# Four graph layers on 128 graphs: bias added in PSUM, scores and attention turned by way of DRAM, a new timetable, and a rearranged start

## The chip, the cores and the metric

The kernel runs on one core of a Trainium2 chip. The engines are TensorE (PE, with PEld for its weight loads), VectorE (DVE), ScalarE (ACT), GpSimd (POOL) and SyncE (SP), which here only issues DMAs. Each engine takes its own instructions in order and waits on semaphores for the others. The metric is the device time of one execution in microseconds (us), lower is better.

## The reference

`x` is 128 graphs of 128 nodes with 512 features, `adj` a 128x128 matrix shared by all graphs. Four layers follow each other; each ends in `x = layernorm(x + layer(x))` over the features.

```python
# layer 0
y = einsum('nm,bmd->bnd', adj, x);  out = y @ W0 + bias
# layer 1
q, k, v = x @ Wq.T, x @ Wk.T, x @ Wv.T
rel = adj.T * (q @ k.T);  rel /= norm(rel, axis=2);  out = rel @ v
# layer 2
h = x @ W2;  s1, s2 = h @ a1, h @ a2
e = leaky_relu(s1[:, :, None] + s2[:, None, :], 0.2) * adj
out = elu(softmax(e, axis=2) @ h + beta * h)
# layer 3 (with W1 = W2 = adj the row's own term drops out of the difference C - A)
out = relu(max over features of adj @ x + b)        # one number per node
```

All of it is in fp32.

## The kernel before, in words

The 128 graphs are handled in 32 groups of G = 4. For each group the kernel makes the same chain of steps, and the steps of about four groups are interleaved. The order is written out by hand: every step is handed to `emit(at, f)` with a time in slots, `TABLE` (lines 231 to 246) gives the times of a group, 28 slots apart from group to group, `FIRST` (248) changes them for groups 0 and 1 and `LAST` (250) for groups 29, 30 and 31. At the end all pieces are sorted by their time (line 826) and called in that order. So the table sets the order of the instructions on every engine; no scheduler moves them afterwards, and each engine works through its queue in that order.

Names in the profile, with the steps that make them:

- `load` reads a group's `x` (tile x1). `aggregate` multiplies by `adjT` (p_y) and ScalarE copies the result to yT.
- `product` (339) multiplies a group's 512x512 block matrix by a weight matrix with seven products of half-size blocks instead of eight (two by two blocks, sums of blocks as factors). The sums on the data side (s_y, s_x, s_z) are made by GpSimd in `left_factors` (294), those of the weights once, by VectorE, in `weight_blocks` (143). The seven steps go in `ORDER = (1, 2, 6, 5, 7, 3, 4)`; their results lie in three PSUM regions, r0 (two buffers) and r1 and r2, which share one buffer (tag r12). After each step `out` (359) drains the region: a copy by ScalarE or an addition by VectorE. A region is added to by the next step of its number, so that step waits for the drain. Four products of this kind are made per group: r_y (layer 0), r_m (x times Wq^T Wk, layer 1), r_v (layer 1) and r_z (layer 2).
- `biased` (434): GpSimd adds the bias row to x1, so that the drains of r_y add onto it.
- `turn_blocks` and `move` transpose x for layer 1: VectorE transposes 32x32 blocks (xB), and 16 DMAs put the blocks in place (xT). Groups 0 and 1 use TensorE (`turn`, p_xT) instead. `turn_rel` and `move_rel` do the same with the masked scores (relB, relT).
- `scores` (p_rel), `masked`, `squares`, `inverse`, `attend` (p_o), `residual`: the rest of layer 1. `dots` and `scale_dots` compute the two dot products of layer 2 for each node (d12).
- `spread` (623): four TensorE transposes (p_s) put the second dot product of every node on all partitions. `leaky` (632), `weighted` (643, GpSimd), `greatest` (646), `exps` (650, ScalarE), `divide` (662, GpSimd multiplies by the reciprocal): the softmax. `turn_att` (669): four TensorE transposes (p_eT); `with_beta` (675) adds beta times the identity and writes eT. `gather` (685): p_z from x2 and eT.
- `exp`, `elu`, `widen` (p_a), `top`, `norm`, `store`: the end of layer 2 and layer 3.

PSUM tiles of whole banks (p_y, p_rel, p_z and so on) share three buffers (`bank`, line 82).

Before group 0 the weights are loaded, W0, the bias and W2 by ACT's DMA queue, the rest by SP's. `prepare_qk` (163) computes Wq^T Wk with 16 plain 128x512 products (p_m), `prepare_v` (178) transposes Wv (p_wv), and `prepare_dots` (188) and `prepare_rows` (202) make the rows for the two dot products (col, wa).

Of the kernel before, what the change touches and what calls it, by code (L numbers as in the profile page):

```python
# [8 lines left out]
FP = mybir.dt.float32  # L9
# [20 lines left out]
def kernel(  # L30
# [32 lines left out]
    nc = tc.nc  # L63
# [8 lines left out]
    G = 4  # L72
    NG = B // G
    assert B % G == 0 and K == 4

# [3 lines left out]
    small = ctx.enter_context(tc.tile_pool(name="small", bufs=4))  # L79
    psum = ctx.enter_context(tc.tile_pool(name="psum", bufs=1, space=bass.MemoryType.PSUM))  # L80

    def bank(name):
        return psum.tile([P, D], FP, tag="ps", name=name, bufs=3)
# [21 lines left out]
    bias_sb = const.tile([P, D], FP)  # L105
    nc.scalar.dma_start(bias_sb, on_all(bias0, D))

# [34 lines left out]

    def weight_blocks(w, name, keep=0):


        def blk(kh, ch):
            return w[:, 2 * kh : 2 * kh + 2, H * ch : H * ch + H]

        t = const.tile([P, 3 + keep, 2, H], FP, name=f"t_{name}")
        t2, t3, t4 = t[:, 0], t[:, 1], t[:, 2]  # L150
        t1 = t[:, 3] if keep else blk(0, 1)
        dve.tensor_tensor(t3, blk(1, 1), blk(0, 1), ALU.subtract)
        dve.tensor_tensor(t2, t3, blk(0, 0), ALU.add)
        dve.tensor_tensor(t4, blk(1, 0), t2, ALU.subtract)
        dve.tensor_tensor(t1, blk(0, 1), blk(0, 0), ALU.subtract)
        return {1: blk(0, 0), 2: blk(1, 0), 3: blk(1, 1), 4: t4, 5: t1, 6: t2, 7: t3}

    bw = {}

    def prepare_0():  # L160
        bw["0"] = weight_blocks(w0_sb, "0")

    def prepare_qk(c):

        pm = bank(f"p_m{c}")
        for e in range(K):
            pe.matmul(
                pm,
                wq_sb[:, e, c * P : (c + 1) * P],
                wk_sb[:, e, :],  # L170
                start=(e == 0),
                stop=(e == K - 1),
            )
        act.copy(m_qk[:, c, :], pm)
        if c == K - 1:
            bw["m"] = weight_blocks(m_qk, "m")

    def prepare_v(c):
        pv = bank(f"p_wv{c}")
        for e in range(K):  # L180
            pe.transpose(pv[:, e * P : (e + 1) * P], wv_sb[:, e, c * P : (c + 1) * P], ident)
        act.copy(wvT[:, c, :], pv)
        if c == K - 1:
            bw["v"] = weight_blocks(wvT, "v")

# [27 lines left out]

    def prepare_2():
        bw["2"] = weight_blocks(w2_sb, "2", 1)


# [9 lines left out]
    def row(at, step, n=G):  # L227
# [110 lines left out]

    def product(at, name, mul, s, w, c, fresh, begin=None):


        r = {}

        def step(i):
# [4 lines left out]
            if first:  # L349
                r[where] = psum.tile(  # L350
                    [P, 2, H],
                    FP,
                    tag="r0" if where == 0 else "r12",
                    name=f"r{where}_{name}",
                    bufs=2 if where == 0 else 1,
                )
            mul(r[where], s["f"][i], bw[w][i], first)
# [7 lines left out]

        for n, i in enumerate(ORDER):
            emit(at[n], step, i)
            emit(at[n] + 0.72, out, i)
# [46 lines left out]
    def layer0(g, t):  # L415
# [24 lines left out]
        each(t["bias"], biased)  # L440
        left_factors(t["y_sums"], s, "yT", "s_yz", f"y_{g}", 0)
        product(t["y_w"], f"y_{g}", by_rows, s, "0", rows_of(lambda: x1[g]), False)
        each(t["stats0"], lambda b: stats(s, f"0_{g}", b, x1[g][:, b, :]))
# [176 lines left out]
    def layer2(g, t):  # L620
        s = {}

        def spread():
            s["p"] = bank(f"p_s2_{g}")
            for b in range(G):
                pe.transpose(
                    s["p"][:, b * P : (b + 1) * P],
                    s12[g][:, 1, b : b + 1].to_broadcast([P, P]),
                    ident,
                )  # L630

        def leaky():
            e = work.tile([P, G, P], FP, tag="e", name=f"e_{g}")
            dve.tensor_tensor(
                e,
                s["p"].rearrange("p (b n) -> p b n", b=G),
                s12[g][:, 0, :, None].to_broadcast([P, G, P]),
# [24 lines left out]
        def divide(i):  # L662
            rs = small.tile([P, n], FP, tag=f"rs{n}", name=f"rs_{g}_{i}")
            dve.reciprocal(rs, s["sums"][:, i * n : i * n + n])
            e = s["e"][:, i * n : i * n + n, :]
            engine = pool if n == G else dve
            engine.tensor_tensor(e, e, rs[:, :, None].to_broadcast([P, n, P]), ALU.mult)
# [7 lines left out]
        def with_beta(i):  # L675
            if i == 0:
# [5 lines left out]
                ALU.add,  # L682
            )

        def gather(b):
# [52 lines left out]
        each(t["divide"], divide)  # L738
        each(t["turn_att"], turn_att)
        each(t["with_beta"], with_beta)  # L740
        each(t["gather"], gather)
# [115 lines left out]
```

## Time and profile before

| | |
|---|---|
| time, three runs | 2218.19, 2218.97, 2220.17 us |
| the profiled run, and its span | 2217.06 us, 2214.6 us |
| busy: PE, DVE, ACT, POOL | 2170.9, 1547.9, 1102.5, 907.7 us |
| 16 DMA engines, q1 | 19.7% |
| granted TensorE clock, mean | 0.996 |
| GpSimd's bias additions | x128, 1331 ns each |
| TensorE transposes p_s and p_eT | x128 each |

Busy times are unions: two instructions of one engine that overlap count once. A matmul on fp32 data appears as two records, a transpose as one. Spans of matmuls include the way through the array and so overlap; what one costs in a row is the distance from start to start. In a timeline the columns are the start in us, the length in us, engine, line, operation, output and inputs, shapes and the number of instructions that were merged; brackets give the idle time of the engine just before and what ended it.

### The profile page before, as it was taken

To read this page: it belongs to the slowest core of one execution; us is meant where nothing else is said; L and a number is where in the kernel's file an instruction comes from. 1 tells how busy PE (TensorE), PEld (TensorE's weight loads), DVE (VectorE), ACT (ScalarE), POOL (GpSimd) and SP (SyncE) were. 2 spreads that over 40 slices of the span, in tenths; PEclk is the share of its full clock that TensorE was granted. 3 is DMA by queue.
4 is the path that set the end of the run, shared out by engine and by line. 5 is a ranking of instruction groups with operands and counts; after the bars stand their busy time and mean duration, and the time that the engine had idled before them with its cause. 6 is when DMAs were issued, how large, how long until landed. Compare 5 with 4: busy or idle time off the path is not lost.

```text
span 2214.6 us, 31863 instructions
## 1 busy us (share of the span) xinstructions
PE 2170.9 (98%) x11073; PEld 1839.6 (83%) x11073; DVE 1547.9 (70%) x3290; ACT 1102.5 (50%) x2446; POOL 907.7 (41%) x743
## 2 busy tenths in 40 slices
PE   7999999999999999999999999999999999999996
PEld 5788888888888888888888888888888888888873
DVE  4657766767766767776767776767767677667676
ACT  2224445554445554445554445554455554455547
POOL 3334444334444344443344443344443344443321
PEclk9999999999999999999999999999999999999998
DMA  4011222211222211222112222112222112221101
GB/s 167 25 20 29 61 60 62 62 20 49 60 60 63 58 21 52 59 61 62 44 31 56 58 62 63 41 30 59 58 62 63 29 39 62 59 63 44 21 28 57
DMA packets 333295, 115.15 MB, mean 52 GB/s; under 512 B 297424, under 2 KB 297552, under 8 KB 333136
## 3 DMA queue, kind: packets, MB, share of 16 engines
q1 hardware_dynamic: 331936, 110.77, 19.7%
q10 hardware_dynamic: 1200, 2.36, 0.3%
q8 instruction: 88, 1.44, 0.3%
q14 instruction: 71, 0.58, 0.1%
HBM read 39.65 MB, written 33.55 MB: 33 GB/s over the span
## 4 chain that ended last, share of the span: by engine, by line
PE 93%; DVE 3%; ACT 2%; POOL 1%; issue 1%; DMA 0%; ACTq 0%; DVEq 0%; POOLq 0%
PE r_y L26 17%; PE r_v L26 17%; PE r_m L26 17%; PE r_z L26 17%; PE p_z L26 5%; PE p_rel L26 5%; PE p_y L26 5%; PE p_o L26 5%; PE p_a L26 5%; DVE x L26 1%; ACT x L26 1%; DVE st L26 1%; PE p_eT L26 1%; PE p_m L26 1%; PE p_s L26 1%
## 5 line engine op out<-in xcount | busy, mean ns | idle before, releaser
L26 ACT ACTIVATE x<-x,nmean,rstd 128x512 f32<-128x512 f32 x384 | 288.6, 808 | 120.8 <-DVE nmean L26 120.8
L26 DVE BATCH_NORM_STATS2 st<-x 128x6 f32<-128x512 f32 x384 | 263.8, 687 | 8.8
L26 POOL TENSOR_TENSOR x<-x,bias_sb 128x512 f32<-128x512 f32 x128 | 170.1, 1331 | 137.9 <-PE p_y L26 137.5
L26 DVE SCALAR_TENSOR_TENSOR x<-m,x 128x512 f32<-128x512 f32 x128 | 114.4, 894 | 108.5 <-ACT m L26 98.5
L26 POOL TENSOR_TENSOR s_x<-xT 128x512 f32<-128x512 f32 x64 | 82.2, 1285 | 261.1 <-DMA xT<-xB 250.2
L26 ACT COPY c<-r_z 128x512 f32<-128x512 f32 x124 | 71.2, 574 | 223.3 <-PE r_z L26 198.0
L26 ACT COPY yT<-p_y 128x512 f32<-128x512 f32 x128 | 75.1, 586 | 213.6 <-PE p_y L26 213.6
L26 POOL TENSOR_TENSOR rstd<-ve,mhalf 128x4 f32<-128x4 f32 (+1 forms) x99 | 98.5, 995 | 194.1 <-DVE ve L26 188.9
L26 DVE TENSOR_TENSOR x<-r_y,x 128x512 f32<-128x512 f32 x224 | 151.7, 678 | 31.2 <-PE r_y L26 31.0
L26 DVE SCALAR_TENSOR_TENSOR scr<-x,wa 128x512 f32<-128x512 f32 x256 | 161.5, 675 | 0.0
L26 DVE STREAM_TRANSPOSE xB<-x 128x512 f32<-128x512 f32 x120 | 81.2, 696 | 108.7 <-ACT x L26 97.7
L26 PEld LDWEIGHTS p_y<-adjT,x 128*128 128x128 f32 x1024 | 136.9, 196 | 11.2 <-ACT adjT L26 4.8
L26 POOL TENSOR_TENSOR s_z<-zT 128x512 f32<-128x512 f32 x31 | 39.4, 1270 | 255.9 <-ACT zT L26 255.9
L26 PE MATMUL p_y<-adjT,x 128*128 128x128 f32 x1024 | 137.6, 280 | 4.5 <-ACT adjT L26 4.5
L26 PEld LDWEIGHTS p_z<-eT,x 128*128 128x128 f32 x1024 | 134.0, 192 | 7.9 <-issue 1.0
L26 PEld LDWEIGHTS p_rel<-xT,tT 128*128 128x128 f32 x1024 | 134.1, 191 | 7.4 <-DVE tT L26 0.8
L26 DVE TENSOR_REDUCE mx<-p_a 128x1 f32<-128x512 f32 x128 | 88.3, 691 | 69.6 <-PE p_a L26 69.6
L26 PE MATMUL p_a<-x,adjT 128*128 128x512 f32 x256 | 130.8, 596 | 5.8 <-DVE mx L26 4.4
L26 ACT COPY tT<-r_m 128x512 f32<-128x512 f32 x128 | 75.6, 590 | 121.6 <-PE r_m L26 121.6
L26 PE MATMUL p_rel<-xT,tT 128*128 128x128 f32 x1024 | 134.9, 275 | 0.6 <-DVE tT L26 0.6
L26 PE MATMUL p_z<-eT,x 128*128 128x128 f32 x1024 | 134.7, 275 | 0.1
L26 PE MATMUL p_o<-v,relT 128*128 128x512 f32 x256 | 130.4, 593 | 0.3 <-ACT v L26 0.3
(129 smaller groups left out, 5268.6 us busy)
## 6 DMA issues: line engine op xcount, KB each, us to landing
out_dram<-x SPq DMA_DIRECT2D x128, 256.0 KB, 2.5
x<-in_x_dram SPq DMA_DIRECT2D x31, 1024.0 KB, 5.3
xT<-xB SPq DMA_DIRECT2D x480, 64.0 KB, 2.3
relT<-relB SPq DMA_DIRECT2D x512, 16.0 KB, 1.8
w_sb<-in_L_gnn_weight_dram ACTq DMA_DIRECT2D x1, 1024.0 KB, 5.6
x<-in_x_dram SPq DMA_DIRECT2D x4, 256.0 KB, 7.8
wq_sb<-in_L_gnn_Wq_dram SPq DMA_DIRECT2D x1, 1024.0 KB, 12.3
wk_sb<-in_L_gnn_Wk_dram SPq DMA_DIRECT2D x1, 1024.0 KB, 15.1
```

The costliest lines, as they stand in the source:

```text
L26: return lambda *args, **kw: self.tc.keep_in_program_order(op(*args, **kw))
```

## The change

What it does:

1. **Bias.** `biased` is gone. Two ScalarE copies per group (`fill`) put the bias into regions r0 and r2 before the first step that writes there (0.7 slots before steps 1 and 5), and these steps add onto it. `bias_sb` holds the left half of the bias and the right half less the left. Three opening matmuls write each region's buffers once.
2. **Scores.** For groups 0 to 29 `spread` writes the column of d12 to DRAM and reads it back on all partitions (s2d, s2), two DMAs on SP, in place of p_s. Groups 30 and 31 keep TensorE.
3. **Attention.** For groups 0 to 29 `divide` is done by VectorE with beta added in the same instruction, four per group; a block transpose (eB), one DMA to DRAM and four DMAs back (eT) take the place of p_eT and `with_beta`.
4. **New times** for y_sums, spread to divide, exp to store, and the first two groups.
5. **The fill.** The bias and W2 are loaded by SP's queue. VectorE copies adjT. Eight warm-up matmuls. Wq^T Wk is made by `product`, with factors of wk (t_k) and wq (s_q). The factors of the weights are emitted one by one at times of their own, those of W2 earlier; xT of group 0 and the transposes of Wv are interleaved.

The diff, cut to its core:

```diff
-    nc.scalar.dma_start(bias_sb, on_all(bias0, D))
+    nc.sync.dma_start(bias_sb, on_all(bias0, D))
...
-    nc.scalar.dma_start(w2_sb, w2.rearrange("(k p) f -> p k f", p=P))
+    nc.sync.dma_start(w2_sb, w2.rearrange("(k p) f -> p k f", p=P))
...
+    bias_halves = {0: bias_sb[:, :H], 2: bias_sb[:, H:]}
+    dve.tensor_tensor(bias_halves[2], bias_halves[2], bias_halves[0], ALU.subtract)
     ident = const.tile([P, P], FP)
     make_identity(nc, ident)
+    for tag, n in (("r0", 2), ("r12", 1)):
+        for i in range(n):
+            r = psum.tile([P, 2, H], FP, tag=tag, name=f"first_{tag}_{i}", bufs=n)
+            pe.matmul(r, ident, ident[:, None, :].to_broadcast([P, G, P]), start=True, stop=True)
     mhalf = const.tile([P, G], FP)
     dve.memset(mhalf, -0.5)
 
     adjT = const.tile([P, P], FP)
     pt = bank("p_adjT")
     pe.transpose(pt[:, :P], adj_sb, ident)
-    act.copy(adjT, pt[:, :P])
+    dve.tensor_copy(adjT, pt[:, :P])
+    warm = bank("p_warm")
+    for i in range(WARM):
+        pe.matmul(warm[:, :P], ident, ident, start=True, stop=True)
     adj_b = adj_sb[:, None, :].to_broadcast([P, G, P])
     adjT_b = adjT[:, None, :].to_broadcast([P, G, P])
 
...
-        load=[-20], y=row(0.5, 1), bias=row(1.3, 1), y_sums=row(5.2, 0.5), y_w=row(7, 1, 7),
+        load=[-20], y=row(0.5, 1), y_sums=row(4.3, 0.5), y_w=row(7, 1, 7),
...
-        spread=[61.6], leaky=[62.0], weighted=[63.4], greatest=[64.3], exps=[64.4],
-        divide=[65.8], turn_att=[68.6], with_beta=[69.0], gather=row(71.5, 1),
-        z_sums=row(75.3, 0.5), z_w=row(77, 1, 7), exp=[87.5, 88.5, 90.4, 92.0],
-        elu=[87.8, 89.4, 92.8, 93.8], norm2=[95.0], apply2=row(95.7, 0.33),
-        widen=[98.7, 100.0, 103.6, 104.6], top=[99.1, 100.4, 104.0, 105.0],
-        stats3=[99.8, 101.1, 104.7, 105.7], norm3=[106.2], apply3=row(107, 0.33), store=[108.5],
+        spread=[57.3], leaky=[62.6], weighted=[62.9], greatest=[63.9], exps=[64.0],
+        divide=[65.2], turn_att=[68.6], with_beta=[69.0], turn_blocks_2=[65.7], move_2=[65.8], gather=row(71.5, 1),
+        z_sums=row(75.3, 0.5), z_w=row(77, 1, 7), exp=[86.0, 87.0, 96.0, 99.6],
+        elu=[86.4, 87.4, 96.8, 100.3], norm2=[101.4], apply2=row(102.4, 0.33),
+        widen=[104.2, 104.9, 105.6, 106.3], top=[104.7, 105.4, 106.1, 106.8],
+        norm3=[107.4], apply3=row(108.4, 0.33), store=[109.8],
     )
 
...
-    FIRST = {0: dict(turn=row(20.4, 0.3)), 1: dict(y=row(-9.5, 0.3), bias=row(-9.2, 0.3))}
+    FIRST = {
+        0: dict(stats0=row(15.8, 0.02), norm0=[15.95], apply0=row(18.0, 0.1), turn=row(20.4, 0.3)),
+        1: dict(y=row(-9.5, 0.3), turn=row(20.3, 0.3), x_sums=row(22.5, 0.5)),
+    }
...
+        def fill(where):
+            r[where] = region(where)
+            act.copy(r[where], before[where][:, None, :].to_broadcast([P, 2, H]))
...
+            if first and before is not None and where in before:
+                first = False
+            elif first:
+                r[where] = region(where)
...
+            if before is not None and i in (1, 5):
+                emit(at[n] - 0.7, fill, REGION[i])
...
-        def biased(b):
-            pool.tensor_tensor(x1[g][:, b, :], x1[g][:, b, :], bias_sb, ALU.add)
...
+                line = dram.tile([P, G], FP, tag="s2", name=f"s2d_{g}")
+                sync.dma_start(line, s12[g][:, 1, :])
+                wide = work.tile([P, P, G], FP, tag="s2", name=f"s2_{g}")
+                sync.dma_start(
+                    wide.rearrange("p n b -> p (n b)"),
+                    line.rearrange("n b -> (n b)")[None, :].to_broadcast([P, P * G]),
+                )
...
+            if not late:
+                for b in range(G):
+                    e = s["e"][:, b, :]
+                    dve.scalar_tensor_tensor(
+                        e, e, rs[:, b : b + 1], beta_i, op0=ALU.mult, op1=ALU.add
+                    )
+                return
...
+        def turn_blocks():
+            s["eB"] = work.tile([P, Q, G, P // Q], FP, tag="eB", name=f"eB_{g}")
+            dve.transpose(
+                s["eB"].rearrange("p q b u -> p b q u"),
+                s["e"].rearrange("p b (q u) -> p b q u", q=Q),
+            )
+
+        def move():
+            m = P // Q
+            blocks = dram.tile([P, Q, G * m], FP, tag="eB", name=f"eBd_{g}")
+            sync.dma_start(blocks, s["eB"].rearrange("p q b u -> p q (b u)"))
+            eT = work.tile([P, Q, G, m], FP, tag="eT", name=f"eT_{g}")
+            for q in range(Q):
+                sync.dma_start(
+                    eT[q * m : (q + 1) * m].rearrange("p a b u -> p a (b u)"),
+                    blocks.rearrange("(a j) q n -> q j a n", a=Q)[q],
+                )
+            s["eT"] = eT.rearrange("p a b u -> p b a u")
...
-    emit(-1, prepare_0)
-    each(row(14.0, 1.0), prepare_qk)
-    each(row(18.0, 0.1), prepare_v)
-    each(row(29.2, 1.8), prepare_dots)
-    emit(40.7, prepare_rows)
-    emit(61.0, prepare_2)
+    weight_blocks(row(-1, 0), "0", w0_sb)
+    weight_blocks([11.85, 11.86, 12.85, 12.86], "k", wk_sb, 1, "x2")
+    qk = {"qT": wq_sb}
+    left_factors(row(12.0, 0.1), qk, "qT", "s_x", "q", 1)
+    product(row(14, 1, 7), "qk", by_rows, qk, "k", rows_of(lambda: m_qk), True)
+    weight_blocks([19.8, 19.81, 20.9, 20.91], "m", m_qk)
+    each(row(21.0, 0.1), prepare_v)
+    weight_blocks(row(29.8, 0.01), "v", wvT)
+    each([33.8, 34.2, 43.8, 44.8], prepare_dots)
+    emit(49.0, prepare_rows)
+    weight_blocks(row(48.9, 0.01), "2", w2_sb, 1)
```

In 'late' groups (30 and 31) `spread`, `turn_att` and `with_beta` are as before.

More of the change, by code (lines that the diff above doesn't have):

```diff
@@ L73 @@
     NG = B // G
+    WARM = 8
     assert B % G == 0 and K == 4
@@ L80 @@
     psum = ctx.enter_context(tc.tile_pool(name="psum", bufs=1, space=bass.MemoryType.PSUM))
+    dram = ctx.enter_context(tc.tile_pool(name="dram", bufs=2, space=bass.MemoryType.DRAM))
     def bank(name):
@@ L141, with weight_blocks, factor @@
     beta_b = beta_i[:, None, :].to_broadcast([P, G, P])
-    def weight_blocks(w, name, keep=0):
+    def weight_blocks(at, key, w, keep=0, tag=None):
         def blk(kh, ch):
             return w[:, 2 * kh : 2 * kh + 2, H * ch : H * ch + H]
[L149 to L156, printed above, removed]
-    bw = {}
[L160 to L176, printed above, removed]
+        t = {}
+        def factor(i):
+            if i == 0:
+                home, args = (const, {}) if tag is None else (data, dict(tag=tag))
+                u = home.tile([P, 3 + keep, 2, H], FP, name=f"t_{key}", **args)
+                t.update({2: u[:, 0], 3: u[:, 1], 4: u[:, 2]})
+                t[1] = u[:, 3] if keep else blk(0, 1)
+                bw[key] = {
+                    1: blk(0, 0), 2: blk(1, 0), 3: blk(1, 1), 4: t[4], 5: t[1], 6: t[2], 7: t[3],
+                }
+            to, left, op, right = (
+                (3, blk(1, 1), ALU.subtract, blk(0, 1)),
+                (2, t[3], ALU.add, blk(0, 0)),
+                (4, blk(1, 0), ALU.subtract, t[2]),
+                (1, blk(0, 1), ALU.subtract, blk(0, 0)),
+            )[i]
+            dve.tensor_tensor(t[to], left, right, op)
+        for i in range(4):
+            emit(at[i], factor, i)
+    bw = {}
     def prepare_v(c):
@@ L182, in prepare_v @@
         act.copy(wvT[:, c, :], pv)
-        if c == K - 1:
-            bw["v"] = weight_blocks(wvT, "v")
     col = const.tile([P, 2, K], FP)
@@ L212, in prepare_rows @@
         dve.tensor_scalar(beta_i, ident, beta_sb, None, op0=ALU.mult)
-    def prepare_2():
-        bw["2"] = weight_blocks(w2_sb, "2", 1)
     pieces = []
@@ L239 @@
         apply1=row(65.4, 0.33),
-        spread=[61.6], leaky=[62.0], weighted=[63.4], greatest=[64.3], exps=[64.4],
-        divide=[65.8], turn_att=[68.6], with_beta=[69.0], gather=row(71.5, 1),
-        z_sums=row(75.3, 0.5), z_w=row(77, 1, 7), exp=[87.5, 88.5, 90.4, 92.0],
-        elu=[87.8, 89.4, 92.8, 93.8], norm2=[95.0], apply2=row(95.7, 0.33),
-        widen=[98.7, 100.0, 103.6, 104.6], top=[99.1, 100.4, 104.0, 105.0],
-        stats3=[99.8, 101.1, 104.7, 105.7], norm3=[106.2], apply3=row(107, 0.33), store=[108.5],
-    )
-    FIRST = {0: dict(turn=row(20.4, 0.3)), 1: dict(y=row(-9.5, 0.3), bias=row(-9.2, 0.3))}
+        spread=[57.3], leaky=[62.6], weighted=[62.9], greatest=[63.9], exps=[64.0],
[4 more added lines that the diff above has]
+        norm3=[107.4], apply3=row(108.4, 0.33), store=[109.8],
+    )
+    FIRST = {
+        0: dict(stats0=row(15.8, 0.02), norm0=[15.95], apply0=row(18.0, 0.1), turn=row(20.4, 0.3)),
+        1: dict(y=row(-9.5, 0.3), turn=row(20.3, 0.3), x_sums=row(22.5, 0.5)),
+    }
     LAST = {
@@ L337, in by_columns, with product, region @@
                 )
-    def product(at, name, mul, s, w, c, fresh, begin=None):
+    def product(at, name, mul, s, w, c, fresh, begin=None, before=None):
         r = {}
+        def fill(where):
+            r[where] = region(where)
+            act.copy(r[where], before[where][:, None, :].to_broadcast([P, 2, H]))
+        def region(where):
+            return psum.tile(
+                [P, 2, H],
+                FP,
+                tag="r0" if where == 0 else "r12",
+                name=f"r{where}_{name}",
+                bufs=2 if where == 0 else 1,
+            )
         def step(i):
@@ L348, in step @@
             first = i in (1, 2, 5)
[L349 to L356, printed above, removed]
+            if first and before is not None and where in before:
+                first = False
+            elif first:
+                r[where] = region(where)
             mul(r[where], s["f"][i], bw[w][i], first)
@@ L439, in layer0 @@
         each(t["y"], aggregate)
-        each(t["bias"], biased)
         left_factors(t["y_sums"], s, "yT", "s_yz", f"y_{g}", 0)
-        product(t["y_w"], f"y_{g}", by_rows, s, "0", rows_of(lambda: x1[g]), False)
+        product(
+            t["y_w"], f"y_{g}", by_rows, s, "0", rows_of(lambda: x1[g]), False, before=bias_halves
+        )
         each(t["stats0"], lambda b: stats(s, f"0_{g}", b, x1[g][:, b, :]))
@@ L621, in layer2 @@
         s = {}
+        late = g >= NG - 2
         def spread():
[L624 to L629, printed above, removed]
+            if late:
+                p = bank(f"p_s2_{g}")
+                for b in range(G):
+                    pe.transpose(
+                        p[:, b * P : (b + 1) * P],
+                        s12[g][:, 1, b : b + 1].to_broadcast([P, P]),
+                        ident,
+                    )
+                s["s2"] = p.rearrange("p (b n) -> p b n", b=G)
+            else:
+                line = dram.tile([P, G], FP, tag="s2", name=f"s2d_{g}")
[4 more added lines that the diff above has]
+                    line.rearrange("n b -> (n b)")[None, :].to_broadcast([P, P * G]),
                 )
+                s["s2"] = wide.rearrange("p n b -> p b n")
         def leaky():
@@ L635, in leaky @@
                 e,
-                s["p"].rearrange("p (b n) -> p b n", b=G),
+                s["s2"],
                 s12[g][:, 0, :, None].to_broadcast([P, G, P]),
@@ L664, in divide @@
             dve.reciprocal(rs, s["sums"][:, i * n : i * n + n])
+            if not late:
+                for b in range(G):
+                    e = s["e"][:, b, :]
[3 more added lines that the diff above has]
+                return
             e = s["e"][:, i * n : i * n + n, :]
@@ L683, in with_beta @@
             )
+        def turn_blocks():
[3 more added lines that the diff above has]
+                s["e"].rearrange("p b (q u) -> p b q u", q=Q),
+            )
+        def move():
[7 more added lines that the diff above has]
+                    blocks.rearrange("(a j) q n -> q j a n", a=Q)[q],
+                )
+            s["eT"] = eT.rearrange("p a b u -> p b a u")
         def gather(b):
@@ L738, in layer2 @@
         each(t["divide"], divide)
-        each(t["turn_att"], turn_att)
-        each(t["with_beta"], with_beta)
+        if late:
+            each(t["turn_att"], turn_att)
+            each(t["with_beta"], with_beta)
+        else:
+            emit(t["turn_blocks_2"][0], turn_blocks)
+            emit(t["move_2"][0], move)
         each(t["gather"], gather)
```

## The prediction

> **What bounds the kernel now.** I read the page's busy times first, then its chain of waits, then one period by the windows view and the timeline, and last the timeline of the first 130 us. The page, parts 1 and 4:
>
> ```profile
> PE 2170.9 (98%) x11073; PEld 1839.6 (83%) x11073; DVE 1547.9 (70%) x3290; ACT 1102.5 (50%) x2446; POOL 907.7 (41%) x743
> ...
> PE 93%; DVE 3%; ACT 2%; POOL 1%; issue 1%; DMA 0%; ACTq 0%; DVEq 0%; POOLq 0%
> ```
>
> TensorE is busy nearly always, and the chain that ends last runs on it. An average over stages can mislead, so here is one period (a group of four batch elements), by engine, in the middle of the run:
>
> ```profile
> core 0: us, PE busy (x) PEld busy (x) DVE busy (x) ACT busy (x) POOL busy (x), PEclk, DMA share, GB/s
> ...
> 922.29:989.10 66.81, 66.81 (x345) 57.15 (x344) 48.65 (x102) 34.22 (x76) 28.14 (x24) 1.00 0.21 52
> ```
>
> 66.81 us of 66.81: no idle time on TensorE at full clock, 18 us of idle on VectorE, 32 on ScalarE. The sum agrees: 28 steps of the four seven-product multiplications start 1.727 us apart (48.4), twelve 128-column blocks take 0.89 (10.7), eight 512-column ones 0.86 (6.9), two sets of transposes 0.437 (0.9). So in the steady part only work taken from TensorE, or a new wait put on it, counts. The two sets are these, each read from its own start to the next start (the 0.60 includes the pipeline's drain):
>
> ```profile
> 920.78 0.60 PE L26 MATMUL p_s<-ident,d 128*128 128x128 f32 x4
> 921.22 1.89 PE L26 MATMUL r_m<-xT,t_m 128*128 128x256 f32 x8
> ...
> 802.60 0.60 PE L26 MATMUL p_eT<-ident,e 128*128 128x128 f32 x4
> 803.04 1.89 PE L26 MATMUL r_y<-t,yT 128*128 128x256 f32 x8
> ```
>
> The fill is different: there TensorE waits, and what it waits for is in brackets.
>
> ```profile
> 8.41 6.55 PE L26 MATMUL p_y<-adjT,x 128*128 128x128 f32 x32 [4.46 <-ACT adjT L26]
> ...
> 56.70 1.99 PE L26 MATMUL r_m<-s_x,t_m 128*128 128x256 f32 x8 [2.00 <-POOL s_x L26]
> ...
> 112.25 2.97 PE L26 MATMUL r_m<-s_x,m_qk 128*128 128x256 f32 x8 [4.39 <-DVE tT L26]
> ...
> 125.61 1.99 PE L26 MATMUL r_y<-w_sb,yT 128*128 128x256 f32 x8 [1.46 <-DVE tT L26]
> ```
>
> **The Trainium skill.** "TensorE: Matmul & The Clock Gate", Part 1: the array runs at half rate until it has been busy for about 3.4 us, and falls back after such a time idle. The trace agrees: the first 32 records take 6.55 us where later ones take 3.6, and after the 4.39 us wait eight records take 2.97 instead of 1.89. "SBUF — State Buffer", Who interferes with whom: a VectorE instruction with two SBUF inputs and a GpSimd one that reads SBUF exclude each other for a whole instruction. It agrees:
>
> ```profile
> 852.69 1.27 POOL L26 TENSOR_TENSOR s_y<-s_y,yT 128x512 f32<-128x512 f32 x1
> 852.82 1.69 DVE L26 SCALAR_TENSOR_TENSOR x<-c,x 128x512 f32<-128x512 f32 x1
> ```
>
> 1.69 instead of 0.68. [...] the page shows 1.8 to 2.5 for 16 to 256 KB. "PSUM — Partial Sum Buffer", The four PSUM rules: ScalarE writes do not change the bits that decide whether a matmul adds or overwrites; a matmul adds to ScalarE's data where an earlier one left the bit set. That is what the three opening matmuls are for; the trace before has no such case.
>
> **The change, part by part (steady state).**
> Scores and attention by DRAM, for groups 0 to 29: 2 x 30 sets x 0.437 us leave TensorE, 26.2 us. Nothing else on TensorE changes per group.
> The scores' way now: a write of 2 KB and a broadcast read of 256 KB on SP, about 2 x 2.5 us, so 5 from the end of the d12 row. That row ends 11.0 us before the group's first y step (call that moment 0; every time in the next paragraphs is relative to it), so the row is back at -6; its reader, leaky, stands behind the last two tT adds and cannot start before -0.9. Hidden, with 5 us to spare. On SP it stands behind four output stores and ahead of the load for a later group (20 slots early) and of the attention's DMAs; none of these is due.
> The attention's way: on VectorE four scalar_tensor_tensor of 128x128 (about 0.28 each, the nearest row is relB at 0.283) and one 32x32-block transpose (0.70, row xB) come, the eT add (0.67) goes: +1.2 us. GpSimd loses its multiply (1.05). On SP one 256 KB write whose landing the next four reads wait for: 2.5, then four issues of 0.65 and 2.3 to land, 7.4 us. The transpose ends at about 8.2, so eT is there at 15.6; p_z wants it at 19.1. Behind it on SP stand the sixteen relT moves, due when VectorE has relB at 13.9, while SP is through at 13.3. Hidden.
> Bias into PSUM: 4 GpSimd adds per group (5.3 us) go, two ScalarE copies (0.58 each, as c<-r_z) come. ScalarE is at half load. The first fill stands early (-3.9). The second is the edit's risk: it waits for VectorE to drain region 1 after step 2 (done 4.6), and in ScalarE's order it is behind the four exps, which wait for greatest, which waits for GpSimd's weighted, which waits for leaky. Worked out: tT done -0.9; leaky's first op now has two SBUF inputs and is shut out by yT until -0.55, then to 0.05; its second is shut out by s_y and ends at 1.85; weighted 3.2; greatest 4.0; exps (1.65) 5.75; fill 6.4. TensorE wants it after y1, y2, p_rel, y6, p_rel: 3 x 1.727 + ... = 6.96. So 0.5 us spare, and TensorE loses nothing. With both shut-outs at full length it is 6.9: at worst some 0.1 us. Bounds for this edit: 0 to +0.6 per group (a gain is excluded, since TensorE has no idle time to give).
> New times: p_a and elu move; after v, p_a, z and o I find every drain ahead of its next writer, the nearest being v's fifth step, copied at 27.1 for the step at 27.9. Zero.
>
> **The fill.** (Absolute times.) bias_sb moves from ACT's queue to SP's, behind x; the last x landed at 10.71 with the same bytes ahead, so take bias at 10.7. VectorE subtracts its halves (0.35), and only then copies adjT: p_y starts near 11.5, not 8.41. If the eleven warm-up matmuls keep the clock up it takes 3.6 us: 15.1, against 14.8. ScalarE then puts the last yT and the fill (2 x 0.59) ahead of y: 16.4. Seven steps: 28.5 against 27.84. Wq^T Wk: 7 x 1.727 = 12.1 for 13.7; p_y of group 1 (3.6) now lies inside it, and covers the additions for t_m; then transposes of x and Wv through three banks, paced by eight ScalarE copies: 48.7. Then m without the 2.0 us wait: 60.8, against 65.44. y of group 1 15.7, v 12.1 plus a wait of some 1.6 (v's fifth copy behind three normalisations on ScalarE), xT, wa and p_o 6.1: 96.3 against 99.83. Then group 1's m meets the long VectorE chain of group 0's residuals and dots as before (15.0 us from the first residual to tT); without GpSimd's bias adds the three small d operations need 0.6 instead of 3.7, so 12, from 94: TensorE waits 2.7, not 4.39, and likely keeps its clock. y of group 2 starts near 115, against 122.25, of which 0.44 is a transpose already counted: 6.8. The 1.46 us wait in it came from w2's factors, now made earlier: 1.4 more. Fill: -8.2; bounds +2 (p_y cold, every bank wait longer) to -13.
> The end of the run (from 2109 on) keeps its order of work: 0, at most 2 either way.
>
> **Sum.** 2214.6 - 26.2 - 8.2 = 2180.2 us for the span. That profiled execution was 2217.06 as a run, and the three runs have the median 2218.97, 4.4 above the span; so 2185.
>
> **Rivals.** (A) The fill gains nothing: late p_y, cold clock, and ScalarE as pacemaker take back what the shorter products give. For it: p_y does start 3 us later. Then 2219 - 26 = 2193.
> (B) The second fill comes late by a little in every group: 0.3 to 0.6 us x 30 = 9 to 18: 2194 to 2203. For it: four engines in a row with half a microsecond to spare. Against it: in the trace before the same chain from leaky to exps repeats within 0.1 us from group to group.
> (C) Slower, one mechanism: the same fill at y5, with leaky delayed enough (its strided read of the row s2, or the lock lost twice more). Price: each period loses what the chain is late beyond 0.5 us. It decides from 0.5 + 34/30 = 1.65 us on; at 2.1 us late TensorE waits 1.6 x 30 = 48: 2185 + 48 = 2233. Against it: p_s is read at 0.68 and the SBUF transposes with strided sides show no surcharge (0.70).
> (D) The scores never get off TensorE's path, since the DRAM round trips take over 10 us in place of 5 to 7: p_z or leaky would wait, the transposes' saving is eaten, 2215 to 2222. Against it: 2.5 us landings at 20% DMA share.
>
> **How the numbers follow.** My forecast 0.60, A 0.12, B 0.13, C 0.12, D 0.03. What the measurement can tell from no change is 0.2%, 4.4 us. Faster: forecast, A and B, 0.85; D gives 0.02 of same and 0.01 of slower; C 0.12: slower 0.13. The range: the fill's good bound gives 2180 less some in the tail, so 2174 below; above through A and B to 2204. C and D stay out, 0.15.
>
> **What would show it.** Right: period 65.93 with TensorE without idle time; no p_s or p_eT before group 30; POOL busy near 700 us, ACT near 1140; r_y's fifth-product step without a wait for ACT. Wrong: a bracket "<-ACT r_y" on that step in every group (B, C); p_z waiting for DMA eT (D); y of group 2 starting after 120 (A).

## The result, and the profile after

The changed kernel takes 2187.68 us (median of four runs, 2185.98 to 2189.60) against 2218.58 for the kernel before: ratio 0.986, 95% interval 0.9843 to 0.9877. The forecast was 2185. The two runs near 2186 were granted 0.996 of the clock and the two near 2189.5 were granted 0.994 and 0.995, so a difference of 2 to 4 us between medians is read below together with the traces. The profiled execution ran 2189.29 us with a span of 2187.4, 27.2 less than before. Its page, parts 1 and 4 (the lines of the kernel before are in the prediction):

```profile
PE 2152.3 (98%) x10879; PEld 1823.8 (83%) x10879; DVE 1557.2 (71%) x3419; ACT 1127.9 (52%) x2509; POOL 722.4 (33%) x589
...
PE 94%; DVE 3%; ACT 1%; issue 1%; DMA 0%; POOL 0%; SPq 0%; ACTq 0%; DVEq 0%
```

TensorE has 18.6 us less busy time and the same share of it; GpSimd has lost 185 us and ScalarE gained 25. One period by the windows view, from the y of one group to the y of the next:

```profile
core 0: us, PE busy (x) PEld busy (x) DVE busy (x) ACT busy (x) POOL busy (x), PEclk, DMA share, GB/s
908.13:974.09 65.96, 65.96 (x338) 56.40 (x337) 47.51 (x106) 34.99 (x78) 22.50 (x19) 1.00 0.27 65
```

65.96 us where it was 66.81: the two sets of transposes (2 x 0.437 = 0.87) are gone. Over the 28 periods from group 3 on the mean is 66.04: ten are 66.17 to 66.25, one is 66.07 and the others are 65.93 to 65.97. What lengthens the ten is the subject of experiment 10.

Below, "the second fill" is ScalarE's second copy of the bias into PSUM, while "the fill" alone is the start of the run, before the periods become regular. The steps of a product go in the order 1, 2, 6, 5, 7, 3, 4; "the fourth product" counts in this order, so it is step 5.

The second fill is the place within the period that could have gone wrong, here from the timeline of TensorE and of ScalarE:

```profile
912.48 1.89 PE L26 MATMUL r_y<-t,s_y 128*128 128x256 f32 x8
915.10 1.89 PE L26 MATMUL r_y<-w_sb,s_y 128*128 128x256 f32 x8
...
913.81 0.57 ACT L26 COPY r_y<-bias_sb 128x512 f32<-128x512 f32 x1
```

The second fill ends at 914.38 and the step that adds onto it starts at 915.10 with no bracket: 0.72 us to spare. And the start of the run, on TensorE:

```profile
5.94 1.95 PE L26 MATMUL p_warm<-ident 128*128 128x128 f32 x16
11.48 5.47 PE L26 MATMUL p_y<-adjT,x 128*128 128x128 f32 x32 [3.60 <-DVE adjT L26]
18.12 3.72 PE L26 MATMUL r_y<-w_sb,yT 128*128 128x256 f32 x16 [1.17 <-ACT r_y L26]
...
109.42 2.46 PE L26 MATMUL r_m<-s_x,m_qk 128*128 128x256 f32 x8 [2.71 <-DVE tT L26]
111.67 1.92 PE L26 MATMUL p_y<-adjT,x 128*128 128x128 f32 x8
...
118.98 3.62 PE L26 MATMUL r_y<-w_sb,yT 128*128 128x256 f32 x16
```

The warm-up is over at 7.9; then TensorE stands idle for 3.60 us until VectorE has copied adjT, and p_y takes 5.47 us, not 3.6. After the 2.71 us wait in group 1's m, eight p_y records take 1.92 where they take 1.05 elsewhere: half the clock again (the view of this stretch is in the last section). So y of group 2 begins at 118.98 (before: 122.25).

The span's 27.2 us by place: up to the y of group 3, 5.88, of which 1.31 are transposes and 4.57 the fill; the 28 periods after it, 22.26; the end of the run 0.95 the other way. Of the edits of the fill, experiments 8 and 9 test the order of adjT and the warm-up; what each of the others gives, no run separates.

### The profile page after: what moved, and what is told of

It is laid out like the page before. It is cut to its first block, busy times and chain, and to the rows that moved or that the text cites. A ratio compares the mean times of both kernels' runs of the same rounds, so it can differ in the third digit from the quotient of the medians.

```text
span 2187.4 us, 32020 instructions
## 1 busy us (share of the span) xinstructions
PE 2152.3 (98%) x10879; PEld 1823.8 (83%) x10879; DVE 1557.2 (71%) x3419; ACT 1127.9 (52%) x2509; POOL 722.4 (33%) x589
## 3 DMA queue, kind: packets, MB, share of 16 engines
q10 hardware_dynamic: 528, 1.05, 0.1%
## 4 chain that ended last, share of the span: by engine, by line
PE 94%; DVE 3%; ACT 1%; issue 1%; DMA 0%; POOL 0%; SPq 0%; ACTq 0%; DVEq 0%
PE r_y L26 18%; PE r_v L26 17%; PE r_m L26 17%; PE r_z L26 17%; PE p_y L26 5%; PE p_z L26 5%; PE p_rel L26 5%; PE p_o L26 5%; PE p_a L26 5%; DVE x L26 1%; ACT x L26 1%; DVE st L26 1%; PE r_qk L26 1%; DMA bias_sb<-in_L_gnn_bias_dram 0%; DVE scr L26 0%
## 5 line engine op out<-in xcount | busy, mean ns | idle before, releaser
L26 POOL TENSOR_TENSOR rstd<-ve,mhalf 128x4 f32<-128x4 f32 (+1 forms) x99 | 109.1, 1102 | 340.1 <-DVE ve L26 340.1
L26 ACT ACTIVATE x<-x,mean,r 128x512 f32<-128x512 f32 x128 | 97.1, 808 | 109.0 <-DVE mean L26 109.0
L26 POOL TENSOR_TENSOR rn<-n,mhalf 128x4 f32<-128x4 f32 x32 | 32.6, 1019 | 348.3 <-ACT sq L26 348.3
L26 DVE TENSOR_TENSOR tT<-r_m,tT 128x512 f32<-128x512 f32 x96 | 66.3, 691 | 102.7 <-PE r_m L26 98.3
L26 ACT COPY zT<-p_z 128x512 f32<-128x512 f32 x128 | 73.9, 577 | 118.9 <-PE p_z L26 118.9
L26 POOL TENSOR_TENSOR s_y<-yT 128x512 f32<-128x512 f32 x32 | 41.0, 1281 | 281.3 <-ACT yT L26 281.3
L26 PE MATMUL p_a<-x,adjT 128*128 128x512 f32 x256 | 126.3, 597 | 5.8 <-DVE mx L26 4.4
L26 ACT COPY v<-r_v 128x512 f32<-128x512 f32 x128 | 74.2, 580 | 104.2 <-PE r_v L26 104.2
```

The source lines that it names most:

```text
L26: return lambda *args, **kw: self.tc.keep_in_program_order(op(*args, **kw))
```

## Experiments

The kernel before was measured beside each, with medians of 2218.2 to 2218.6, so that medians of different experiments can be set side by side; ratios are to the kernel before.

**1. Both ways back on TensorE.**

```
-        late = g >= NG - 2
+        late = True
```
(and `spread` at 61.6 as before)

> The changed kernel with scores and attention turned on TensorE again in all groups (two sets of transposes a group), the rest as changed. Theory: the steady part is TensorE's sum of work, so 30 x 2 x 0.437 = +26.2 us over the changed kernel, about 2214 us; the period is 66.9 us. Rival (the gain of the steady part came from the times or from the bias in PSUM, the transposes lay in gaps): 2187 to 2192 us and a period of 66.0 to 66.2.

Measured: 2214.43 us, ratio 0.9979 (0.9970 to 0.9989), mean period 66.96. That is 26.7 us above the changed kernel, 26.2 forecast. It also shows what everything else in the change is worth together: 4.0 us (2.4 to 6.7 by the interval).

**2. The scores alone back on TensorE.**

```
-            if late:
+            if True:
```
(in `spread`, at 61.6)

> The changed kernel with the scores alone turned on TensorE again, the attention still by way of DRAM. Theory: the two ways are worth the same, 0.437 us a group each, +13.1 us over the changed kernel, about 2201 us, period 66.4 to 66.5. Rival 1 (the DRAM way of the scores delays leaky and with it the second fill, and costs back what it saves): 2188 us or less. Rival 2 (one way carries the whole gain): 2188 or 2214 us.

Measured: 2201.21 us, ratio 0.9922 (0.9906 to 0.9939), mean period 66.47: 13.5 us above the changed kernel, half of the 26.7. The two ways add, and neither takes anything back.

**3. The bias by GpSimd again.**

```
+        def biased(b):
+            pool.tensor_tensor(x1[g][:, b, :], x1[g][:, b, :], bias_sb, ALU.add)
...
+        each(t["bias"], biased)
-            t["y_w"], f"y_{g}", by_rows, s, "0", rows_of(lambda: x1[g]), False, before=bias_halves
+            t["y_w"], f"y_{g}", by_rows, s, "0", rows_of(lambda: x1[g]), False
```
(the times of these additions and of the y sums as before, and no subtraction of the bias halves)

> The changed kernel with the bias added by GpSimd to x again (4 adds a group, 5.3 us), and no fill of PSUM; DRAM ways, times and start as changed. Theory: TensorE has no idle time in the steady part, so the bias edit is worth nothing there; without the fill ahead of y the first product starts up to 1 us sooner: 2184 to 2192 us. Rival (the lock between GpSimd's adds and VectorE's two-input work was what the times needed relief from): elu and residuals come late, TensorE waits, 2197 us or more.

Measured: 2189.38 us, ratio 0.9869 (0.9855 to 0.9884), which overlaps the changed kernel's interval; mean period 66.07. GpSimd is busy 892 us and VectorE 1633 (76 more for one instruction fewer: the lock with GpSimd's additions), and TensorE does not feel it in the periods. In the start the edit has both signs: here p_y starts at 8.65, since adjT stands behind no bias, and the wait in group 1's m is 4.83 us, since GpSimd's additions are back in the way (two d<-mv,wa_sum,d of 128x4 ahead of tT take 2.46 us beside them, 0.35 in the changed kernel); y of group 2 begins at 118.37, within 0.6 us of the changed kernel.

**4. The kernel before with the DRAM ways alone.** `spread`, `divide` and `layer2` as in the change, the attention's block transpose at 66.3 and its DMAs at 66.4; bias, all other times and the start as before.

> The kernel before with the DRAM ways of scores and attention alone; its bias adds, times and start stay. Theory: the transposes leave whatever the times are, 30 x 2 x 0.437 = 26.2 us: 2192 to 2198 us. Rival (the DRAM ways need the new times or the bias relief, since VectorE's extra 1.2 us a group meets GpSimd's lock): period of 66.5 or more, 2205 to 2219 us.

Measured: 2269.12 us, ratio 1.0228 (1.0212 to 1.0243): 50.7 us slower than before, outside both expectations. The period is 68.42 at least, and in nearly every group one step waits. The timeline of VectorE, and the step of TensorE that waits; below them the start of a group's y and the same drain in the kernel before:

```profile
951.06 0.68 DVE L26 TENSOR_TENSOR x<-r_y,x 128x512 f32<-128x512 f32 x1
951.66 0.68 DVE L26 SCALAR_TENSOR_TENSOR x<-c,x 128x512 f32<-128x512 f32 x1
952.44 0.69 DVE L26 SCALAR_TENSOR_TENSOR x<-m,x 128x512 f32<-128x512 f32 x1
...
954.18 1.14 DVE L26 SCALAR_TENSOR_TENSOR e<-e,rs,beta_i 128x128 f32<-128x128 f32 x4
955.36 0.71 DVE L26 STREAM_TRANSPOSE eB<-e 128x512 f32<-128x512 f32 x1
955.99 0.65 DVE L26 TENSOR_TENSOR x<-r_y,x 128x512 f32<-128x512 f32 x1
...
956.79 0.45 PE L26 MATMUL r_y<-w_sb,s_y 128*128 128x256 f32 x1 [1.86 <-DVE ve L26]
```

```profile
922.95 3.62 PE L26 MATMUL r_y<-w_sb,yT 128*128 128x256 f32 x16
...
933.18 0.66 DVE L26 TENSOR_TENSOR x<-r_y,x 128x512 f32<-128x512 f32 x1
```

The last two x<-r_y,x are the third and fourth drains of y. The sixth product adds to the region that the fourth one drains; the bracket names ve, the small instruction right behind that drain. Counted from this group's y (942.33), that drain starts at 13.66; in the kernel before it starts at 10.23 (933.18 less 922.95), and TensorE gets to the step at 12.20. Of the 3.43 us, 1.5 are there from the first drain on (leaky's first operation, whose two inputs now both come from SBUF, takes 1.78 us beside GpSimd's sum instead of 0.68), and 1.9 are the four multiplies and the block transpose. An elu step of the layer behind, x<-c,x and x<-m,x with its statistics, stands between the same two drains.

**5. The same with the times of exp to store.**

```
-        z_sums=row(75.3, 0.5), z_w=row(77, 1, 7), exp=[87.5, 88.5, 90.4, 92.0],
-        elu=[87.8, 89.4, 92.8, 93.8], norm2=[95.0], apply2=row(95.7, 0.33),
+        z_sums=row(75.3, 0.5), z_w=row(77, 1, 7), exp=[86.0, 87.0, 96.0, 99.6],
+        elu=[86.4, 87.4, 96.8, 100.3], norm2=[101.4], apply2=row(102.4, 0.33),
```
(and widen to store as in the change)

> The kernel before with the DRAM ways alone, as in the run that was slower, and of the new times only those from exp to the store of layer 3 (two of the four elu steps, 2.1 us of VectorE each with their statistics, leave the stretch between the drains of y). Theory: in the slower run VectorE's drain ahead of y's sixth product came 3.5 us later than before, 2.0 us of it for the attention's multiplies and block transpose, 1.5 for the lock on leaky; with one elu less ahead of it the drain fits again, TensorE has no wait, and the transposes' 26 us appear: 2190 to 2198 us, period 66.0. Rival (the lock on leaky, or the order of leaky to divide, is what counts): the period stays over 67.3, 2230 us or more.

Measured: 2197.87 us, ratio 0.9905 (0.9890 to 0.9920), mean period 66.04. That is 20.7 below the kernel before and not the full 26: in the profiled executions the periods give 22.2, while y of group 3 starts 4.0 later than before and the end takes 1.0 more. The same stretch:

```profile
924.82 1.14 DVE L26 SCALAR_TENSOR_TENSOR e<-e,rs,beta_i 128x128 f32<-128x128 f32 x4
...
926.63 0.69 DVE L26 TENSOR_TENSOR x<-r_y,x 128x512 f32<-128x512 f32 x1
...
929.94 1.89 PE L26 MATMUL r_y<-w_sb,s_y 128*128 128x256 f32 x8
```

The multiplies are still ahead of the fourth drain, the elu step isn't; the drain starts at 8.89 after this group's y (917.74), and the sixth product at 12.20 without waiting. The lock is still there (leaky's two operations take 1.92 and 1.60 us). So 71 us lie between experiments 4 and 5, and they differ in the places of exp, elu and layer 3 alone. That the two elu steps are what counts among these is read from the two timelines; no run moves them by themselves.

**6. The same with the other half of the times.**

```
+        y_sums=row(4.3, 0.5), spread=[57.3], leaky=[62.6], weighted=[62.9], greatest=[63.9], exps=[64.0]
+        divide=[65.2], turn_blocks_2=[65.7], move_2=[65.8]
```
(in experiment 4's kernel, with exp to store as before)

> The kernel before with the DRAM ways alone and of the new times only those of the y sums and of spread to the attention's block transpose; exp, elu and layer 3 keep their old times. Theory: the elu steps still stand between the drains of y, so the drain ahead of y's sixth product is still 1 to 1.9 us late in every group: period 67.2 to 68.4, 2228 to 2265 us. Rival (these times are what the DRAM ways need): period 66.0, 2190 to 2198 us.

Measured: 2261.44 us, ratio 1.0196 (1.0179 to 1.0213), period 68.29. The multiplies have moved one drain ahead, and with them the wait, from the sixth product to the fifth:

```profile
949.88 1.96 PE L26 MATMUL r_y<-t,yT 128*128 128x256 f32 x8 [1.48 <-DVE x L26]
```

**7. The second fill's copy three times.**

```
-            act.copy(r[where], before[where][:, None, :].to_broadcast([P, 2, H]))
+            for _ in range(3 if where == 2 else 1):
+                act.copy(r[where], before[where][:, None, :].to_broadcast([P, 2, H]))
```

> The changed kernel with the second fill's copy made three times (2 more x 0.59 = 1.18 us on ScalarE ahead of y's fifth step). In the trace the fill ends 0.70 us before TensorE wants it. Theory: TensorE then waits about 0.47 us before that step in each of some 31 groups, +14 to +15 us over the changed kernel, about 2202 us, and the bracket on that step names ScalarE. Rival 1 (what the trace shows as spare isn't: the whole 1.18 us lands on TensorE): +36 us, 2224. Rival 2 (more spare than the trace shows): within 3 us of 2188.

Measured: 2209.36 us, ratio 0.9958 (0.9942 to 0.9975), 21.7 above the changed kernel, mean period 66.72: more than the 14 to 15 expected, less than rival 1.

```profile
989.50 1.82 ACT L26 COPY r_y<-bias_sb 128x512 f32<-128x512 f32 x3
...
991.37 1.99 PE L26 MATMUL r_y<-w_sb,s_y 128*128 128x256 f32 x8 [0.42 <-ACT r_y L26]
```

Three copies take 1.82 where one takes 0.57, 1.25 more; 0.72 were spare, 0.05 pass between the last copy and the step, so the step starts 0.58 late. The next one starts another 0.10 late: 0.68 us a period for a bracket of 0.42. So the spare time of the trace was real, and this stop of TensorE costs 0.26 us more than its bracket. 0.16 of it lies before the step: the bracket counts from the end of the p_rel records, and those are 1.05 long where the next step otherwise starts after 0.89. 0.10 lies in the step itself, whose records take 1.99 in place of 1.89.

**8. adjT ahead of the bias.** The subtraction of the bias halves goes behind adjT's copy on VectorE.

```
-    dve.tensor_tensor(bias_halves[2], bias_halves[2], bias_halves[0], ALU.subtract)
...
     adjT = const.tile([P, P], FP)
     pt = bank("p_adjT")
     pe.transpose(pt[:, :P], adj_sb, ident)
     dve.tensor_copy(adjT, pt[:, :P])
+    dve.tensor_tensor(bias_halves[2], bias_halves[2], bias_halves[0], ALU.subtract)
```

> The changed kernel with the transposed adjacency copied on VectorE ahead of the subtraction of the bias halves, which waits for bias to land at 10.8 us. Theory: the first p_y starts near 8 us straight after the warm-up, keeps the full clock (3.6 us and not 5.47) and everything after it moves up: about 5 us less than the changed kernel, 2182 to 2184 us. Rival 1 (the landing of x, 10.7 us, and of the weights paces the start): 2186 to 2188 us. Rival 2 (as the kernel before: p_y starts early but cold and waits inside): 1 to 3 us less.

Measured: 2184.30 us, ratio 0.9845 (0.9830 to 0.9860), 3.4 below the changed kernel and just outside the 2182 to 2184 expected. The two intervals overlap; all four runs lie below all four of the changed kernel.

```profile
8.10 3.74 PE L26 MATMUL p_y<-adjT,x 128*128 128x128 f32 x32
...
104.32 3.40 PE L26 MATMUL r_m<-s_x,m_qk 128*128 128x256 f32 x8 [2.72 <-DVE tT L26]
```

p_y runs at full clock, y of group 0 starts 5.1 us sooner and y of group 3 too (176.40 for 181.48). The span of the profiled run is 5.2 shorter: the periods, with a mean of 66.08, take back 1.2 of the 5.1, and the end, of which below, gives 1.4.

**9. The same without p_warm** (`WARM = 0` for 8).

> The kernel with adjacency first (2184.3 us, p_y 3.74 us from 8.10 on), without the eight p_warm matmuls; the six first_r matmuls of 512 columns stay. Theory: first_r alone (5 us) brings the clock up and the gap to p_y stays short enough to keep it, so the p_warm ones are worth nothing: p_y takes 3.7 us, 2184 us. Rival (they keep the clock up): p_y takes 5.5 to 6.6 us, the start of y moves by 0 to 2.5 us, up to 2187 us.

Measured: 2183.90 us, ratio 0.9844 (0.9829 to 0.9859), the same as experiment 8.

```profile
7.22 3.81 PE L26 MATMUL p_y<-adjT,x 128*128 128x128 f32 x32 [1.12 <-DMA x<-in_x_dram]
...
105.51 2.00 PE L26 MATMUL r_m<-s_x,m_qk 128*128 128x256 f32 x8 [2.72 <-DVE tT L26]
```

The three first_r matmuls (six records) bring the clock up and 1.12 us of idle time don't cost it. The p_warm ones are worth nothing that shows here: with adjT first they aren't needed, and in the changed kernel, where 3.60 us of idle time follow them, they did not keep the clock.

**10. Layer 3's shift earlier.** What the ten longer periods lose is seen at z's third region in the changed kernel. All engines between 291.6 and 294.5:

```profile
291.65 1.26 POOL L26 TENSOR_TENSOR s_x<-xT 128x512 f32<-128x512 f32 x1 [1.46 <-PE r_z L26]
...
291.84 1.10 DVE L26 TENSOR_TENSOR mean<-mean,r 128x4 f32<-128x4 f32 x1
...
292.97 0.81 ACT L26 ACTIVATE x<-x,mean,r 128x512 f32<-128x512 f32 x1 [3.98 <-DVE mean L26]
...
293.69 0.56 ACT L26 COPY c<-r_z 128x512 f32<-128x512 f32 x1
...
294.40 0.45 PE L26 MATMUL r_z<-w_sb,s_z 128*128 128x256 f32 x1
```

GpSimd's sum began 0.2 us before VectorE's four-column multiply, which then takes 1.10 us instead of 0.13, its shortest; ScalarE's normalisation waits for that, ScalarE's copy that drains z's region stands behind it, and the step starts 0.15 us after the copy is done, 0.16 late; its own eight records take 1.97 in place of 1.89, which makes some 0.25 together. (The expectation's thirteen of 28 was counted too high.) The edit moves the multiply ahead of a residual on VectorE, and with it the first normalisation on ScalarE:

```
-        norm3=[107.4], apply3=row(108.4, 0.33), store=[109.8],
+        norm3=[107.4], apply3=[107.95, 108.73, 109.06, 109.39], store=[109.8],
```

> The changed kernel with layer 3's first x<-x,mean,r of a group moved ahead on ScalarE's order, so that GpSimd and VectorE meet otherwise before z's third step. Theory: the 0.25 us that TensorE loses before z's third step in 13 of 28 periods come from VectorE's small mean<-mean,r shut out by GpSimd's s_x, with ScalarE's copy of z's region queued behind it; with the order changed they go: 3 us less than the changed kernel, period 65.93 throughout. Rival (another cause, or the meeting just moves to another instruction): within 1 us of the changed kernel, period still 66.0 to 66.1.

Measured: 2183.86 us, ratio 0.9843 (0.9829 to 0.9858), 3.8 below the changed kernel; all periods from group 3 on are 65.93, to 0.01, where the changed kernel has a mean of 66.04: 3.0 us of the gain are the periods. The intervals overlap here too, and what carries the reading is that none of the 28 periods is long any more. The same place:

```profile
290.01 0.16 DVE L26 TENSOR_TENSOR mean<-mean,r 128x4 f32<-128x4 f32 x1
...
290.92 0.56 ACT L26 COPY c<-r_z 128x512 f32<-128x512 f32 x1
...
294.01 0.38 PE L26 MATMUL r_z<-w_sb,s_z 128*128 128x256 f32 x1
```

**11. Three waits of the start and the shift together:** experiments 8 and 10, and in `FIRST`, for group 0 and group 1,

```
+            dots=[51.7, 53.8, 57.8, 58.6], scale=[58.9], spread=[59.0],
...
+        1: dict(y=row(-9.5, 0.3), turn=row(20.3, 0.3), x_sums=row(22.5, 0.5), apply0=row(17.73, 0.1)),
```

> The two edits of the last kernels (adjacency first; layer 3's first shift early) and two more for the start: group 0's last two dots and its scores' spread behind the tT adds that group 1's m waits for 2.71 us, and group 1's first normalisation order, for the 1.25 us wait in v. Theory: the gains add: 5 + 3 + 2.7 + 1.7 (the clock lost after the 2.71 us wait) + 1.25, about 12 to 14 us less than the changed kernel, 2174 to 2176 us. Rival (the start is paced by VectorE's total work in group 0, so a wait taken away returns at the next step): 5 to 8 us less, 2180 to 2183.

Measured: 2176.88 us, ratio 0.9814 (0.9799 to 0.9828), 10.8 below the changed kernel (span 2175.0, 12.4 less), 0.9 above the expected range. The waits of 3.60, 2.71 and 1.25 us are gone; y of group 2 starts at 108.94, 10.0 sooner, y of group 3 at 172.77, 8.7 sooner: 1.3 comes back, part of it as a wait of y's fourth product in group 2 for the second fill (0.68 us), behind scores that now come later.

**12. And one factor of w0 after the first drains:** `weight_blocks([-1, -1, 8.75, -1], "0", w0_sb)` for `row(-1, 0)`.

> The fastest kernel so far (adjacency first, layer 3's first shift early, dots and spread of group 0 late, group 1's first normalisation order) with the third of w0's four factors made after the first two drains of y of group 0, since only y's last product reads it. Theory: VectorE's factors (1.7 us each while GpSimd makes the y sums) hold the first drain back, and with it y's third step (1.73 us of wait); one of them less gives 1.0 to 1.7 us: 2175 to 2176 us. Rival (the time returns at the next wait of the start): 2176.9 as it was.

Measured: 2175.97 us, ratio 0.9807 (0.9793 to 0.9822). The 1.73 us wait in y of group 0 is gone and y of group 3 starts 1.75 us sooner (171.02); the median moves by 0.9, within what two medians can differ by chance. Experiments 11 and 12 are the fastest versions here, 12 with 42.6 us below the kernel before.

## Why the prediction was right, step by step

**What bounds, and the transposes.** Right, and shown: 26.2 us forecast, 26.7 measured by putting both back, 13.5 by one.

**The DRAM trips.** Right that they are hidden. The price came from the profile before, where DMAs of 16 to 256 KB land after 1.8 to 2.5 us, and for the broadcast read of the scores it was too low: 5.1 us to land, not 2.5. From the page, and from the timelines of SyncE and VectorE in the group shown first:

```profile
s<-s2d SPq DMA_DIRECT2D x30, 256.0 KB, 5.1
eBd<-eB SPq DMA_DIRECT2D x30, 256.0 KB, 2.0
eT<-eBd SPq DMA_DIRECT2D x120, 64.0 KB, 2.0
...
896.29 0.33 SPq L26 DMA_DIRECT2D s2d<-d  x1
897.73 0.33 SPq L26 DMA_DIRECT2D s<-s2d  x1
...
907.22 1.30 DVE L26 TENSOR_TENSOR e<-s,d 128x512 f32<-128x512 f32 x1
```

The read waits for the write, which took only 1.4; the row is there at 902.86, and leaky, behind the tT additions, starts at 907.22: 4.4 us spare here and at least 2.4 in all 30 groups (5 forecast). eT lands 4.35 to 6.13 us before p_z in all 30 groups (3.5 forecast).

**Bias into PSUM.** Right: nothing in the steady part (experiment 3), and 0.70 to 0.72 us to spare at the second fill in the steady groups (0.5 forecast). Experiment 7 shows that this number is a true margin. Rivals B and C fall with it.

**New times, "Zero".** As a term of the sum this was short by 3 us, and the step under it failed twice. The claim that every drain is ahead of its next writer missed z's third region: 0.25 us in ten groups, some 3 us in all (experiment 10). I had priced the lock between VectorE and GpSimd where large operations meet and passed over a four-column one, whose own 0.13 us hides what waits for it. And pricing the times at nothing hid what they carry: without them the DRAM ways cost 51 us (experiment 4), and with those of exp to store alone they saved 20.7 (experiment 5). I looked for the rival that ends slower at the second fill; it lay in VectorE's order between two drains of y, where the change had made room before it filled it. Experiments 5 and 6 put the room in the times of exp to store, and the timelines put it on the two elu steps. That the DRAM ways need VectorE's extra 1.2 us a group was in my text; that they come between two drains with 1.3 us of play (the fourth ends at 10.89, the step is due at 12.20) was not.

**The fill.** Direction right, size off: 4.6 us, not 8.2. Two terms failed, both on the clock. "If the eleven warm-up matmuls keep the clock up it takes 3.6 us" did not hold: 3.60 us of idle time lie between, p_y took 5.47, 1.9 more than the 3.6 from start to start that it takes at full clock (as a record 3.74, experiment 8). I had the start of p_y right (11.5 for 11.48); the end of the warm-up I did not work out, though it needs only the identity and adj, which had landed at 3.51 in the trace before. And "2.7, not 4.39, and likely keeps its clock": the wait was 2.71, the clock was lost, 1.8 us from that step to the fourth after it. The other terms held: v's wait 1.25 (1.6 forecast), the 1.46 us wait gone. Of rival A only the cold clock was true, beyond the late p_y that the sum had.

**The end.** 0 forecast, 0.95 more measured, inside the 2 us given. From the last y to the end the kernels here with the new times of exp to store took 155.3 to 157.6 us. The clock divides them: between y and the last 20 us it was half for one stretch of 3.41 us in six of them, the changed kernel among these (from 2141.7 to 2145.1), and they took 156.1 to 157.6; in the other five it was not, and they took 155.3 to 155.4. The kernel before, where it was not either, took 155.9. So the 0.95 us is not a cost of the change.

**The sum.** The span was 2187.4 where 2180.2 was forecast: 3.6 us short in the fill, 3.0 in z's region, 1.0 at the end, less 0.7 for one long period of the kernel before that has gone, make 6.9 of these 7.2. The time was nearer than that, 2.7 us over the forecast, because I had added 4.4 us for the way from the span to the median of the runs; here it is 0.3. So the forecast's closeness owes some of its worth to luck: two errors of opposite sign.

## What to carry to other kernels

When a change carries work off the engine that sets the time, list what the receiving engine has between each pair of deadlines (here the drains of a PSUM region), not its idle time per period: 18 us of idle time on VectorE did not save an order that was 2 us too full in one place. Two edits of which one makes room and the other fills it must be priced as a pair; each alone can have the other sign. And a small instruction can be the dearest on its engine, by the queue behind it: look for tiny operations with a duration far from their usual one.

## What the runs showed of the hardware

- A stop of TensorE costs more than its bracket: 0.26 us on top of 0.42 (experiment 7), and some 0.25 us for each stop at z that is so short that no bracket shows (experiment 10).
- Whether a wait costs the clock depends on where it falls. After the same wait of 2.71 to 2.73 us in group 1's m the eight records took 1.99 us (scores on TensorE), 2.00 (no p_warm), 2.46, 2.62, 2.93, 3.12 and 3.40 in the others, where 1.99 is full clock. In all 14 traces the granted clock changes only at points that lie a whole number of 3.41 us apart, and their places differ from trace to trace (by 0.7 us between the changed kernel's and experiment 10's). From the first stretch at full clock to 20 us before the end, it was half for the next 3.41 us after every such stretch in which TensorE had been idle for 1.93 us or more, and after none at full clock with less than 1.80; in between both occurred. So a wait that is split between two stretches can be survived. First the changed kernel, then the one with the scores on TensorE:

```profile
core 0: us, PE busy (x) PEld busy (x) DVE busy (x) ACT busy (x) POOL busy (x), PEclk, DMA share, GB/s
107.39:110.80 3.41, 1.38 (x6) 1.25 (x7) 1.87 (x8) 0.42 (x1) 0.00 (x0) 1.00 0.02 1
110.80:114.22 3.42, 3.42 (x13) 3.06 (x12) 0.00 (x0) 0.59 (x2) 0.00 (x0) 0.50 0.39 55
...
104.56:107.97 3.41, 1.91 (x13) 1.61 (x11) 3.34 (x12) 1.07 (x2) 1.02 (x1) 1.00 0.64 156
107.97:111.38 3.41, 2.19 (x12) 1.98 (x13) 1.06 (x4) 0.00 (x0) 0.00 (x0) 1.00 0.39 152
111.38:114.80 3.42, 3.42 (x21) 3.08 (x20) 0.69 (x1) 1.57 (x3) 1.95 (x2) 1.00 0.00 0
```

  In the first, 2.03 us of one stretch are idle (3.41 less 1.38 busy) and the next has PEclk 0.50. In the second the wait leaves 1.50 and 1.22 idle in two stretches, and the clock stays. At the start p_y likewise kept its clock after 2.82 us (3.84, both ways on TensorE; 1.36 and 1.46 idle) and lost it after 3.08 (5.47, scores on TensorE; 0.81 and 2.27). The Trainium skill, "TensorE: Matmul & The Clock Gate", Part 1, says that the window over which activity is judged runs freely and isn't started by the kernel, and with that these runs agree; it also puts the fall at about 3.4 us of idle time, and there they differ: a wait of 2.7 us was enough in five of seven. A loss cost some 1.8 us in group 1's m and 1.9 in p_y, as much as some of the edits above are worth.
- VectorE's 128x4 multiply of two SBUF tiles, 0.13 us at its shortest, took up to 1.2 us beside a GpSimd sum; in experiment 10 it ends 0.03 us after the sum does, so the delay there is what was left of the other's instruction.
- A 256 KB read that broadcasts one 2 KB row from DRAM took 5.1 us to land (median of 30), where 256 KB written to DRAM took 2.0. Part of this may be company: in 29 groups SP issues the 1 MB load of a later x 0.4 us behind the read, and in the thirtieth, without one, it took 4.2 (3.9 to 4.2 in experiments 4, 5, 6 and 11).
